# Gated attention in float32: weighted values as products over 32 rows, four heads side by side

## The chip, the cores and the metric

The kernel runs on one core of a Trainium2 chip. The metric is the device time of one execution in microseconds; of several runs the median is taken. TensorE is called PE in the profile (PEld for its weight loads), VectorE DVE, ScalarE ACT, GpSimd POOL, SyncE SP.

## The reference

Four batches of 512 tokens of width 256 go through a layer norm. An attention of 16 query heads over 4 key and value heads (head width 128, causal) and a feed-forward gate (inner width 1024) both read the normed tokens.

```python
xn = layernorm(x)
Q, K, V = xn @ Wq + bq, xn @ Wk + bk, xn @ Wv + bv          # 16, 4, 4 heads of 128
attn = softmax(Q K^T / sqrt(128) + causal mask)
y = gelu(concat_heads(attn @ V) @ Wo + bo)
s = layernorm(xn + y) * gamma + beta
gate, up = split(xn @ w_gate_up^T)
g = silu((silu(gate) * up) @ w_down^T)
out = x + s * g
```

All is float32. Query heads g, g + 4, g + 8, g + 12 share key head g.

## The kernel before, in words

Every float32 operand of TensorE is kept in two parts, hi (rounded) and lo (the exact rest), and a product is three matmuls, hi*hi, hi*lo and lo*hi, summed in PSUM (`product`, L93, its matmuls on L95, L96 and L97). `split_psum` (L82) makes the parts: hi by ACT (L86, or L89 with a bias), lo by DVE (L87, or L90).

The feed-forward gates of all four batches come first (`gate_up`, `down`); their results and the transposed tokens are parked in DRAM. The attention follows. It goes through 64 steps (batch b, key group g, query tile i of 128 queries). For a step, `scores` (L422) makes four tiles of scores: sub-tile t holds 32 queries of each of the four heads of the group on its 128 partitions, and as many keys as they see. DVE takes the negated, masked scores and their minimum out of PSUM (L449), ACT takes the exponential and its sum (L460), DVE the reciprocal of the sum (L473), and POOL scales (L474). `transposed_probs` (L476) turns the probabilities of key tile j on PE: four transposes (L481) into one PSUM bank, which ACT and DVE split (L86, L87) into pT, keys on the partitions. `weighted` (L486) then multiplies the values of key tile j, all 128 keys at once, with pT of four heads and 128 queries (512 columns) into the bank pc, and splits it into ctxT with the values' bias. `projected` (L505) multiplies ctxT by Wo into py, and at the end of a batch `activated` and `finished` do gelu, layer norm, gate and residual. For i = 0 the scores are a single matmul of whole float32 operands, q0 and k0 (`whole`, POOL, L373).

The order of the work is written out: each step collects chunks with a position (scores of the next step, queries of the next group, transposes and weighted values of this step, projection of the step before), sorts them, and emits them in that order. The planner of the framework starts on each engine the first instruction in that order that is ready by its own estimate, so an engine's queue can interleave neighbouring chunks, and from then on the queue is fixed. The last two steps are emitted side by side. All DMAs are issued on SP's queue, in order.

PSUM has eight banks: two for scores (tag "s"), two for transposes ("t"), one for queries, keys and values ("mm"), one for pc ("c"), two for py ("y0", "y1"). SBUF holds ten slots "w" for weights; the values stay in SBUF in two parts (tag "v").

Of the kernel before, what the change touches and what calls it, by code (L numbers as in the profile page):

```python
# [19 lines left out]
S = 32  # queries of a head in a tile of scores  # L20
MASK = -1e9
HIGHEST = 3.4028235e38
TUNE = {'a0': 0.119, 'a1': 0.3, 's0': 0.673, 's1': 0.335, 't0': 0.293, 't1': 0.231, 'w0': 0.519, 'w1': 0.5, 'o0': -0.076, 'o1': 0.537, 'gelu_at': (0, 1), 'gelu_pos': 0.0, 'fin_g': 1, 'fin_pos': 0.616, 'gelu_behind': 'ctx', 'qd': (1, 2, 1, 0), 'l0': 0.295, 'l1': 0.095, 'l2': 0.234, 'end': {'tab': -1.229, 'T1': 0.136, 'W1': 0.362, 'T0': 0.1, 'W0': 1.019, 'Ob': 0.072, 'Obs': 0.05, 'O1': 0.6, 'O1s': 0, 'O0': 1.0199999999999998, 'key': 'ctx', 'keyb': 'pT', 'G3': 0.1, 'F3': 0.101, 'Gb': 0.5, 'Fb': 0.65, 'vec': True}}
# [3 lines left out]
def kernel(  # L27
    ctx: ExitStack,
    tc: tile.TileContext,
    x: bass.AP,  # [B, L, D]  # L30
    wq: bass.AP,  # [D, H*E]
    bqT: bass.AP,  # [E, H]
    wk: bass.AP,  # [D, KV*E]
    bkT: bass.AP,  # [E, KV]
    wv: bass.AP,  # [D, KV*E]
    bvT: bass.AP,  # [E, KV]
    wo: bass.AP,  # [H*E, D]
    bo: bass.AP,  # [D]
    gamma: bass.AP,  # [D]
    beta: bass.AP,  # [D]  # L40
    wguT: bass.AP,  # [D, 2*INTER]
    wdT: bass.AP,  # [INTER, D]
    out: bass.AP,  # [B, L, D]
):
    """Products of float32 operands run on the tensor engine as products of two
    parts each: hi, rounded to the engine's 12 significant bits, and lo, the exact
    rest. hi*hi + hi*lo + lo*hi, summed in float32, is the float32 product."""
# [6 lines left out]
    G = H // KV  # query heads of a key head: g, g + KV, ...  # L54
    INTER = wdT.shape[0]
    NT = L // P  # token tiles of a batch
    ND = D // P  # chunks of the model dimension
    NI = INTER // P  # chunks of the inner dimension
# [10 lines left out]
    @contextmanager  # L69
    def behind(*keys):  # L70
        """Queues what the block does behind these instructions on their engines."""
        with ExitStack() as stack:
            for k in keys:
                for ins in latest[k]:
                    stack.enter_context(tc.issue_after(ins.ins))
            yield

# [4 lines left out]
    def split_psum(dst, src, bias=None):  # L82
        """dst[:, 0] = hi, dst[:, 1] = lo of a bank of PSUM (plus a bias per partition)."""
# [9 lines left out]
    def product(out_ap, lhs, rhs, first, last, **kw):  # L93
        """out += lhs^T rhs; lhs and rhs are (hi, lo)."""
        nc.tensor.matmul(out_ap, lhs[0], rhs[0], start=first, stop=False, **kw)  # L95
        nc.tensor.matmul(out_ap, lhs[0], rhs[1], start=False, stop=False, **kw)  # L96
        nc.tensor.matmul(out_ap, lhs[1], rhs[0], start=False, stop=last, **kw)  # L97

    # The power -1/2 of a variance.
    mhalf = const.tile([P, NT], F32, name="mhalf")  # L100
    nc.gpsimd.memset(mhalf, -0.5)
    # Loads the scalar engine's table before it is needed.
# [11 lines left out]
    def load_w(name, views, hi_on=None, lo_on=None):  # L114
        """A slot of 1024 columns of weights, in two parts."""
# [9 lines left out]
        w = work.tile([P, 2, 1024], F32R, tag="w", bufs=10, name=f"w_{name}")  # L125
# [6 lines left out]

    # Probabilities of a query tile: [32 queries of each head of a group, sub-tile of 32
    # queries, keys], the last key that the tile sees in the last column. What a sub-tile
    # doesn't see of the last P keys stays zero.
    p_tiles = [const.tile([P, NT, L], F32, name=f"p{k}") for k in range(2)]

    def clear(p, n):
        for t in range(NT - 1):
            nc.gpsimd.memset(p[:, t, ds(n - P + (t + 1) * S, P - (t + 1) * S)], 0.0)  # L140

    def load_x(b):
        if b < 2:
            t = work.tile([P, NT, D], F32, tag="xT", bufs=2, name=f"x_{b}")
        else:
            t = p_tiles[0][:, ts(b - 2, 2)].rearrange("p a n -> p (a n)").rearrange("p (t d) -> p t d", d=D)
# [9 lines left out]
    # The first tokens and the first weights come in small pieces, in the order of their use.  # L156
# [12 lines left out]
    w_first = work.tile([P, 2, 1024], F32R, tag="w", bufs=10, name="w_gu0")  # L169

    def split_first(f, lo_on=None):
        """The columns of f of the first slot of the gate's weights."""
# [8 lines left out]
    # Keeps the tensor engine busy until the first tokens are there, so that its clock is up by then.  # L181
# [22 lines left out]
    # What the attention phase wants back: the transposed tokens in two parts, and for  # L204
    # the end of a batch the normed tokens, gate * gamma and gate * beta + x.
    xT_dram = [dram.tile([P, ND, 2, L], F32, tag=f"xT{b}", name=f"xT_dram_{b}") for b in range(B)]
    fin_dram = [dram.tile([P, NT, 3, D], F32, tag=f"fin{b}", name=f"fin_dram_{b}") for b in range(B)]

    def normed(b, t):
        xn = work.tile([P, D], F32, tag="xn", bufs=2, name=f"xn_{b}_{t}")  # L210
# [8 lines left out]
    def transposed(b, t):  # L219
        """xT[b][c]: the normed tokens, transposed, of chunk c, in two parts."""  # L220
        if t == 0:
            xT[b] = [pair("pt", 4, f"xT_{b}_{c}") for c in range(ND)]
        xn = [normed(b, t), normed(b, t + 1)]
        pt = psum.tile([P, ND, 2, P], F32, tag="t", bufs=2, name=f"pxt_{b}_{t}")
# [27 lines left out]

    # The last S keys that a tile of scores sees hold the diagonal of each head. Masked
    # before the scores are scaled.
# [41 lines left out]
    ff_tags = [("s", 2), ("s", 2), ("t", 2), ("t", 2), ("mm", 1), ("c", 1)]  # L296
    def h_tiles(b):
        """Places for the eight tiles of a batch among those of the attention phase."""
        if b % 2 == 0 or b + 1 == B:
            for k in range(2 if b % 2 == 0 else 1):  # L300
                t = work.tile([P, G, 2, L], F32R, tag="q", bufs=2, name=f"hq_{b}_{k}")
                yield from (t[:, r] for r in range(G))
        else:
            yield from (pair("k", 4, f"hk_{b}_{k}") for k in range(4))
        if b % 2:
            yield from (pair("v", 5, f"hv_{b}_{k}") for k in range(4))
# [5 lines left out]
    def gate_up(b, f):  # L312
# [3 lines left out]
        for u in range(2):  # L316
            tags = ff_tags if b + 1 < B else ff_tags[:4]
            tag, bufs = tags[n_ff % len(tags)]
            n_ff += 1
            ps.append(psum.tile([P, L], F32, tag=tag, bufs=bufs, name=f"pg_{b}_{f}_{u}"))  # L320
# [15 lines left out]
        h = work.tile([P, L], F32, tag="ctx", bufs=2, name=f"h_{b}_{f}")  # L336
# [24 lines left out]
    kT, vv, qT, probs, pT, ctxT = {}, {}, {}, {}, {}, {}  # L361
    wqs, wos = {}, {}
    q0, k0 = {}, {}
    banks = ["mm", "c"]  # "c" only until the first values are weighted

    def free_bank():
        banks.append(banks.pop(0))
        return banks[-1]

    def whole(dst, t):  # L370
        """The first P columns as they were before they were split: so few columns go
        faster through the tensor engine whole."""
        nc.gpsimd.tensor_tensor(dst, t[:, 0].bitcast(F32), t[:, 1].bitcast(F32), ALU.add)  # L373

    def keys(b, g):
        pk = psum.tile([P, L], F32, tag=free_bank(), bufs=1, name=f"pk_{b}_{g}")
# [372 lines left out]
```

## Time and profile before

| | |
|---|---|
| median of three runs | 681.71 us (680.87 to 683.12) |
| span of the profiled execution, first to last instruction | 679.5 us |
| TensorE busy | 661.7 us, 3996 matmuls, mean granted clock 0.994 |
| VectorE, ScalarE, GpSimd busy | 447.8, 402.6, 273.4 us |
| DMA | 34.73 MB, 15.4% of 16 engines' span |

The page gives the span of the profiled execution; its own time is not listed apart from it, and what lies around the span is taken as the 2.2 us between the span and the median. Busy times are of one engine and overlap between engines. The feed-forward part fills the first 180 us, the attention the rest.

### The profile page before, as it was taken

To read this page: it belongs to the slowest core of one execution; us is meant where nothing else is said; L and a number is where in the kernel's file an instruction comes from. 1 tells how busy PE (TensorE), PEld (TensorE's weight loads), DVE (VectorE), ACT (ScalarE), POOL (GpSimd) and SP (SyncE) were. 2 spreads that over 40 slices of the span, in tenths; PEclk is the share of its full clock that TensorE was granted. 3 is DMA by queue.
4 is the path that set the end of the run, shared out by engine and by line. 5 is a ranking of instruction groups with operands and counts; after the bars stand their busy time and mean duration, and the time that the engine had idled before them with its cause. 6 is when DMAs were issued, how large, how long until landed. Compare 5 with 4: busy or idle time off the path is not lost.

```text
span 679.5 us, 12006 instructions
## 1 busy us (share of the span) xinstructions
PE 661.7 (97%) x3996; PEld 581.6 (86%) x3996; DVE 447.8 (66%) x1337; ACT 402.6 (59%) x956; POOL 273.4 (40%) x490
## 2 busy tenths in 40 slices
PE   7979999999999999999999999999999999999995
PEld 6768888889889888888888898889888988888984
DVE  5864434165766766775787666668867766687867
ACT  4434333253765766677676665957666668576772
POOL 5588130720646423222353232216433323354332
PEclk8999999999999999999999999999999999999998
DMA  7753322211310100000022000002210000032000
GB/s 223 246 191 122 127 81 90 77 47 50 92 31 2 36 29 1 1 0 1 20 76 94 1 0 1 2 1 63 63 62 1 1 2 1 1 93 79 1 1 32
DMA packets 25262, 34.73 MB, mean 51 GB/s; under 512 B 2288, under 2 KB 18544, under 8 KB 25200
## 3 DMA queue, kind: packets, MB, share of 16 engines
q1 hardware_dynamic: 25200, 33.97, 15.4%
q8 instruction: 31, 0.51, 0.3%
q14 instruction: 31, 0.25, 0.1%
HBM read 21.38 MB, written 12.58 MB: 50 GB/s over the span
## 4 chain that ended last, share of the span: by engine, by line
PE 89%; DVE 4%; DMA 4%; issue 1%; ACT 1%; POOL 1%; SPq 0%; ACTq 0%; DVEq 0%; POOLq 0%
PE pt L481 10%; PE pc L96 5%; PE pc L95 5%; PE pc L97 5%; PE pq L95 5%; PE py L97 4%; PE ps L97 4%; PE ps L96 4%; PE pq L97 4%; PE pq L96 4%; PE py L95 4%; PE ps L95 4%; PE py L96 4%; PE pg L97 3%; PE pg L96 3%; PE pg L95 3%
## 5 line engine op out<-in xcount | busy, mean ns | idle before, releaser
L474 POOL TENSOR_SCALAR p<-p,total 128x320 f32<-128x320 f32 (+15 forms) x256 | 127.6, 505 | 195.5 <-DVE total L473 174.9
L460 ACT ACTIVATE p<-p,least 128x320 f32<-128x320 f32 (+15 forms) x256 | 133.2, 522 | 59.7 <-DVE least L449 51.0
L449 DVE CUSTOM_DVE_ANT_0 p<-ps,mask 128x320 f32<-128x320 f32 (+15 forms) x256 | 109.8, 435 | 42.6 <-PE ps L97 17.5
L86 ACT CAST pT<-pt 128x512 fp32r<-128x512 f32 x160 | 89.2, 587 | 60.0 <-PE pt L481 59.2
L87 DVE TENSOR_TENSOR pT<-pt,pT 128x512 fp32r<-128x512 f32 x160 | 106.6, 686 | 25.5 <-ACT pT L86 25.0
L481 PE MATMUL pt<-ident,p 128*128 128x128 f32 x640 | 107.2, 273 | 0.5 <-POOL p L474 0.5
L481 PEld LDWEIGHTS pt<-ident,p 128*128 128x128 f32 x640 | 81.1, 142 | 17.5 <-POOL p L474 0.7
L97 PE MATMUL py<-w_o,ctxT 128*128 128x256 f32 x256 | 73.5, 287 | 0.6 <-DVE ctxT L90 0.6
L95 PE MATMUL py<-w_o,ctxT 128*128 128x256 f32 x256 | 72.9, 285 | 0.1
L96 PE MATMUL py<-w_o,ctxT 128*128 128x256 f32 x256 | 72.1, 281 | 0.0
L96 PE MATMUL pc<-pT,v 128*128 128x512 f32 x160 | 69.1, 432 | 0.0
L95 PE MATMUL ps<-kT,qT 128*128 128x288 f32 (+3 forms) x192 | 68.5, 357 | 0.0
L373 POOL TENSOR_TENSOR q<-qT 128x128 f32<-128x128 f32 x64 | 30.4, 474 | 93.7 <-DVE qT L90 55.8
L95 PE MATMUL pc<-pT,v 128*128 128x512 f32 x160 | 64.5, 403 | 0.1
L97 PE MATMUL pc<-pT,v 128*128 128x512 f32 x160 | 63.2, 395 | 0.0
L473 DVE RECIPROCAL total<-total 128x1 f32<-128x1 f32 x256 | 38.4, 158 | 37.2 <-ACT p L460 35.1
L96 PE MATMUL ps<-kT,qT 128*128 128x288 f32 (+3 forms) x192 | 62.2, 324 | 0.0
L97 PE MATMUL ps<-kT,qT 128*128 128x288 f32 (+3 forms) x192 | 61.7, 322 | 0.0
L90 DVE SCALAR_TENSOR_TENSOR qT<-pq,bq_sb,qT 128x512 fp32r<-128x512 f32 x64 | 47.9, 748 | 15.3 <-ACT qT L89 15.3
L89 ACT ACTIVATE qT<-pq,bq_sb 128x512 fp32r<-128x512 f32 x64 | 44.0, 687 | 20.1 <-PE pq L97 19.6
L90 DVE SCALAR_TENSOR_TENSOR ctxT<-pc,bv_sb,ctxT 128x512 fp32r<-128x512 f32 x64 | 47.8, 747 | 11.1 <-ACT ctxT L89 10.5
L95 PE MATMUL pg<-xT,w_gu 128*128 128x512 f32 (+1 forms) x132 | 50.5, 397 | 3.9 <-DVE h L338 2.5
(127 smaller groups left out, 1567.5 us busy)
## 6 DMA issues: line engine op xcount, KB each, us to landing
fin<-fin_dram SPq DMA_DIRECT2D x16, 384.0 KB, 3.2
xT_dram<-xT SPq DMA_DIRECT2D x8, 512.0 KB, 2.6
fin_dram<-gate SPq DMA_DIRECT2D x16, 256.0 KB, 2.0
xT_again<-xT_dram SPq DMA_DIRECT2D x8, 512.0 KB, 3.9
fin_dram<-xn SPq DMA_DIRECT2D x16, 128.0 KB, 2.4
st_q<-in_wq_dram SPq DMA_DIRECT2D x8, 256.0 KB, 3.2
st_o<-in_wo_dram SPq DMA_DIRECT2D x4, 512.0 KB, 3.9
out_dram<-y SPq DMA_DIRECT2D x16, 128.0 KB, 1.7
```

What stands on the lines that cost most here:

```text
L86: first = nc.scalar.copy(hi, src)
L87: second = nc.vector.tensor_tensor(lo, src, hi.bitcast(F32), ALU.subtract)
L89: first = nc.scalar.activation(hi, src, AF.Identity, bias=bias)
L90: second = nc.vector.scalar_tensor_tensor(lo, src, bias, hi.bitcast(F32), ALU.add, ALU.subtract)
L95: nc.tensor.matmul(out_ap, lhs[0], rhs[0], start=first, stop=False, **kw)
L96: nc.tensor.matmul(out_ap, lhs[0], rhs[1], start=False, stop=False, **kw)
L97: nc.tensor.matmul(out_ap, lhs[1], rhs[0], start=False, stop=last, **kw)
L449: nc.vector.tensor_tensor_reduce(pr, ps[:, :seen], mask[:, L - seen :], scale=-SCALE, scalar=HIGHEST, op0=ALU.add, op1=ALU.min, accum_out= ...
L460: exp = nc.scalar.activation(pr, pr, AF.Exp, bias=least[:, r : r + 1], scale=-1.0, accum_out=total[:, r : r + 1],)
L473: latest["dve"] = [nc.vector.reciprocal(total[:, r : r + 1], total[:, r : r + 1])]
L474: latest["pool"] = [nc.gpsimd.tensor_scalar(pr, pr, total[:, r : r + 1], 1.0, ALU.mult, ALU.mult)]
L481: nc.tensor.transpose(pt[:, :, t], p[:, t, ts(j, P)], ident)
```

## The change

The weighted values are computed without a transpose on PE. DVE turns each 32x32 block of a probability tile in its place, so that the 32 partitions of head r hold 32 keys of head r, with queries as columns. A matmul for one head then contracts over the 32 partitions of that head only, in row group r of the array, and the four heads of the group stand in the four row groups, each with its own PSUM bank. A key tile of 128 keys needs four such chunks c. The values have to lie on the partitions in the same way: 32 keys, the same for each of the four row groups. So they are written to DRAM (`v_dram`) and read back four times, once to each 32 partitions (`values_beside`).

Query tiles are handled in pairs: a step is (b, g, h), with tiles 2h and 2h + 1, and a matmul has 256 columns where both tiles see the key tile and 128 where only the second does. A weighted block has 96 matmuls for h = 0 and 192 for h = 1, all emitted as one chunk.

What moves with it: hi of the turned probabilities is an ACT copy from SBUF, lo is on POOL except for three of ten (i, j), which stay on DVE. The reciprocal is taken once for four sub-tiles and the scaling follows it. q0 comes from PSUM by ACT, and the split of queries covers 384 columns. The probabilities have a place for each query tile index (`p_tiles`). PSUM: the four banks "c" hold the weighted values of both halves; scores, queries, keys and values share the two banks "s". SBUF: twelve slots "w", which also take V beside each other and most of pT; Wq and Wo of a group are split once in batch 0, written to DRAM and read back in the later batches. The last two steps are no longer emitted side by side. Comments and the table of tuned positions are dropped; positions are constants.

```diff
+ON_DVE = ((1, 1), (3, 2), (3, 3))
...
+    banks = psum.tile([P, G, 2, 2 * P], F32, tag="c", bufs=1, name="banks")
...
     def values(b, t):
-        pv = psum.tile([P, KV * E], F32, tag=free_bank(), bufs=1, name=f"pv_{b}_{t}")
+        pv = psum.tile([P, KV * E], F32, tag="s", bufs=2, name=f"pv_{b}_{t}")
...
-        v = pair("v", 5, f"v_{b}_{t}")
+        v = pair("pt", 5, f"v_{b}_{t}")
         split_psum(v, pv)
-        vv[b, t] = v
+        nc.sync.dma_start(
+            v_dram[b][:, ts(t, P)].rearrange("g p s e -> p s g e"),
+            v.bitcast(F32).rearrange("p s (g e) -> p s g e", g=KV),
+        )
+
+    def values_beside(b, g, h):
+        n = L // S // 2
+        vr[b, g, h] = work.tile([P, n, 2, E], F32R, tag="w", bufs=12, name=f"vr_{b}_{g}_{h}")
+        for r in range(G):
+            nc.sync.dma_start(
+                vr[b, g, h][ts(r, S)].rearrange("p c s e -> p c (s e)").bitcast(F32),
+                v_dram[b][g, ts(h, L // 2)].rearrange("(c k) s e -> k c (s e)", k=S),
+            )
...
+        pq = pq.rearrange("p (t n) -> p t n", n=S)
+        nc.scalar.activation(q0[b, g][:, :, r], pq[:, :NT], AF.Identity, bias=bq_sb[:, h : h + 1])
+        split_psum(qT[b, g][:, :, :, r], pq[:, NT:], bq_sb[:, h : h + 1])
...
-        latest["dve"] = [nc.vector.reciprocal(total[:, r : r + 1], total[:, r : r + 1])]
-        latest["pool"] = [nc.gpsimd.tensor_scalar(pr, pr, total[:, r : r + 1], 1.0, ALU.mult, ALU.mult)]
+        if t == G - 1:
+            latest["dve"] = [nc.vector.reciprocal(total, total)]
+            for k in range(NT):
+                normalized(b, g, i, k)
...
     def transposed_probs(b, g, i, j):
         p = probs[b, g, i][0]
-        pt = psum.tile([P, G, NT, S], F32, tag="t", bufs=2, name=f"pt_{b}_{g}_{i}_{j}")
-        for t in range(NT):
-            nc.tensor.transpose(pt[:, :, t], p[:, t, ts(j, P)], ident)
-        t = pair("pt", 4, f"pT_{b}_{g}_{i}_{j}")
-        latest["pT"] = split_psum(t, pt.rearrange("p r t n -> p (r t n)"))[:1]
-        pT[b, g, i, j] = t
...
+        u = work.tile([P, NT, NT, S], F32, tag="u", bufs=3, name=f"pu_{b}_{g}_{i}_{j}")
+        nc.vector.transpose(u, p[:, :, ts(j, P)].rearrange("p t (c k) -> p c t k", k=S))
+        u = u.rearrange("p c t q -> p c (t q)")
+        h = i // 2
+        both = j < 2 * h + 1
...
+        t = pT[b, g, h, j][:, :, :, i % 2 if both else 0]
+        nc.scalar.copy(t[:, 0], u)
+        lo_on = nc.vector if (i, j) in ON_DVE else nc.gpsimd
+        lo_on.tensor_tensor(t[:, 1], u, t[:, 0].bitcast(F32), ALU.subtract)
+
+    def weighted(b, g, h):
+        for j in range(2 * h + 2):
+            t = pT.pop((b, g, h, j))
+            v = vr[b, g, j // 2]
+            first = 0 if j < 2 * h + 1 else 1
+            for c in range(NT):
+                for a, d in ((0, 0), (0, 1), (1, 0)):
+                    for r in range(G):
+                        nc.tensor.matmul(
+                            banks[:, r, h, first * P :],
+                            v[ts(r, S), (j % 2) * NT + c, a],
+                            t[ts(r, S), d, c].rearrange("p i n -> p (i n)"),
+                            start=j == 0 and c == 0 and a == d,
+                            stop=c == NT - 1 and a == 1 and j >= 2 * h,
+                            skip_group_check=True,
+                            tile_position=(r * S, 0),
+                        )
...
+    steps = [(b, g, h) for b in range(B) for g in range(KV) for h in range(2)]
+    steps[-2:] = reversed(steps[-2:])
...
+        if n == 0 and ph + 1 < NPH:
+            for r in range(G):
+                chunks.append((0.05 + 0.15 * r, queries, (*divmod(ph + 1, KV), r)))
+        if n == 1 and ph + 2 < NPH:
+            chunks.append((0.45, keys, divmod(ph + 2, KV)))
...
+                    chunks.append((0.0 + 0.3 * m + 0.075 * t, scores, (nb, ng, i, t)))
+            for m, (i, j) in enumerate(transposed_all[steps[s + 1]]):
+                chunks.append((0.65 + 0.35 * m / len(transposed_all[steps[s + 1]]), transposed_probs, (nb, ng, i, j)))
+        chunks.append((0.7, weighted, (b, g, h)))
+        if n == 1 and ph + 1 < NPH:
+            for m in range(2):
+                chunks.append((0.71, values_beside, (*divmod(ph + 1, KV), m)))
...
+                    chunks.append((0.08 + 0.3 * m + 0.075 * r, projected, (pb, pg, i, r)))
...
+    nc.scalar.activation(warm, mhalf[:, 0:1], AF.Gelu)
+    activated(B - 1, [2, 3])
+    for t in (2, 3):
+        finished(B - 1, t, False)
+    for t in (0, 1):
+        load_fin(B - 1, t)
+        for r in range(G):
+            projected(B - 1, KV - 1, t, r)
+    for t in (0, 1):
+        activated(B - 1, [t])
+        finished(B - 1, t, True)
```

## The prediction

> **What bounds the kernel now.** I read the table of engines first, then the slices, then the windows by stage, then the waits of TensorE, then its timeline.
>
> ```profile
> PE 661.7 (97%) x3996; PEld 581.6 (86%) x3996; DVE 447.8 (66%) x1337; ACT 402.6 (59%) x956; POOL 273.4 (40%) x490
> ...
> PE   7979999999999999999999999999999999999995
> ...
> PEclk8999999999999999999999999999999999999998
> ```
> ```profile
> 180.00:660.00 480.00, 478.94 (x2967) 424.00 (x2966) 340.24 (x1108) 324.79 (x800) 186.18 (x366) 1.00 0.08 25
> ```
> In the window of the attention phase the columns after the length are PE, PEld, DVE, ACT, POOL, clock, DMA share. TensorE (PE) is busy 478.94 of 480 us at full clock; DVE has 71%, ACT 68%, POOL 39%, DMA 8%. So a microsecond taken from PE's stream is worth a microsecond, up to some 140 us, when DVE would be next.
>
> ```profile
> PE pg L95 <- DVE h L338: 2.5, 1, 2.5
> ...
> PE pt L481 <- POOL p L474: 0.5, 1, 0.5
> ```
> These are the waits of PE (total, times, longest): nothing of the attention phase keeps it waiting over 1 us. Any wait that the change adds is a net loss.
>
> A busy PE is not PE's rate, since a matmul lasts longer than the distance to the next. The timeline (start, duration) gives the distances:
>
> ```profile
> 520.18 0.28 PE L95 MATMUL py<-w_o,ctxT 128*128 128x256 f32 x1
> 520.30 0.28 PE L96 MATMUL py<-w_o,ctxT 128*128 128x256 f32 x1
> 520.42 0.28 PE L97 MATMUL py<-w_o,ctxT 128*128 128x256 f32 x1
> 520.54 0.60 PE L481 MATMUL pt<-ident,p 128*128 128x128 f32 x4
> 520.89 0.47 PE L96 MATMUL pc<-pT,v 128*128 128x512 f32 x1
> 521.21 0.40 PE L97 MATMUL pc<-pT,v 128*128 128x512 f32 x1
> 521.44 0.40 PE L95 MATMUL pc<-pT,v 128*128 128x512 f32 x1
> ```
> ```profile
> 545.78 0.27 PE L481 MATMUL pt<-ident,p 128*128 128x128 f32 x1
> 545.81 0.48 PE L95 MATMUL pc<-pT,v 128*128 128x512 f32 x1
> ```
> A 512-wide product takes 0.23 us from start to start, a 256-wide one 0.12 (0.118 over longer stretches), a transpose 0.11 (0.60 for four whose last lasts 0.27). The shortest distance is the last pair: 0.03 us.
>
> **What PE loses.** 640 transposes (L481) by 0.11 are 70 us; the chain's share of 10% of the span says 68. The weighted values (pc) are 480 matmuls by 0.232, 111 us. Together 181 us go.
>
> **What PE gets.** Per key group and batch (16 of them) the first pair of query tiles takes 48 matmuls 256 wide and 48 of 128, the second 144 and 48; in all 3072 and 1536, or 1152 sets of four row groups, 768 wide and 384 narrow. A set multiplies as much as one old matmul of its width: the gain is the transposes alone, if four run as one. No row shows 32 rows. From below: a set costs as much as one full-height matmul, 0.118 or, for narrow ones, 0.11 as transposes do: 90.6 + 42.2 = 133 us, 48 us gained. From above: each matmul with its weight load stands for itself, four times that, 531 us, 350 us lost. Between: the 0.03 row says that a fourth matmul starts 0.09 us after the first, so a set that must end before the next starts lasts 0.118 + 0.09 = 0.21, one that overlaps freely 0.118. I take the middle, 0.16 a set: 184 us, **+3 us against the 181 removed**. PE's work stays as it is, and the transposes' gain is spent on four times the instructions.
>
> The Trainium skill bears on this twice. TensorE: Matmul & The Clock Gate, "Measured speedup vs the span model", gives 3.07 times for four row tiles of 512 columns; with 0.118 that would be 0.154 a set and an estimate of 177 us, 4 us gained. The same page, "The mechanism", says that a weight load overlaps running matmuls only where the row groups differ. If so, a row group's next load (0.11) would follow its own matmul (0.118), 0.23 a wide and 0.22 a narrow set and an estimate of 260 us, 79 us lost. In this trace 256-wide matmuls of all 128 rows follow each other at 0.118, each with a load that lasts 0.19 in the records, so loads do run under matmuls of the same rows; no row here shows either case for 32 rows.
>
> **Changes of shape on PE.** Products of 32 and of 128 rows now alternate. After transposes the first product (0.47 long) delays the next to 0.32 instead of 0.23, but it starts 0.03 after the last transpose instead of 0.11, which makes up for it: no loss. That is the lower end, 0. The upper end is that PE runs empty, 0.28 long less 0.118, 0.16 us a change. Twice a step are 64 changes. But the timeline shows single pc matmuls put between other products, so 300 are possible, 48 us. I take 64 by 0.16, **+10 us**.
>
> **Banks.** Queries, keys, values and scores now share the two banks "s"; before, scores had two and the others one or two. A query's bank is held after its last matmul by the ACT copy of q0 (nearest row: exp of 128x128, 403 ns), by hi on 384 columns (exp 384: 618 ns) and by lo on DVE (748 ns for 512, so some 580): 1.6 us. Meanwhile the other bank lets one score (0.42) and a projection (three times 0.118) run: 0.8 us are uncovered, 64 times, 51 us. What can cover them are the weighted products, if their probabilities are there: then 0. Before, a query held its bank for 0.687 + 0.748 = 1.4 us and no wait of pq is on PE's list, because something else was always ready. I take a third, **+17 us**; ends 0 and 51.
>
> **Other engines.** All in the attention window, against its 480 us. DVE: 112 lo of probabilities by 686 ns go to POOL (-77), 192 reciprocals by 158 (-30), a quarter of 64 qT by 748 (-12); 160 transposes of 32x32 blocks come, priced by the row of the same size from SBUF (w_gu on L112, 680 ns): +109. Bounds: 290 ns (the 128x128 reduction) to 1.05 us (hk on L343), 46 to 168; so 267 to 389 busy, under PE. ACT: probabilities from SBUF cost 620 (row L342) for 587, +5; q0 +26, shorter hi -11: 345. POOL: 64 q0 sums by 474 go (-30), 112 lo by 1.35 us come (w_q on L112): +151, 307. In the first batch splits of weights add four rows a slot, 2 by 0.68 and 2 by 1.4, as now. None is the bound. Probabilities are prepared a step ahead, some 15 us, over DVE, ACT and POOL (0.68 + 0.62 + 1.35 us a block); that step covers them, and I cost them at nothing. Without it the last tile's chain (four by 0.68 on DVE, then 0.62 and 1.35: 4.7 us) would be seen 16 times: 75 us. The single reciprocal makes four normalizations wait for the last exp; they stand in the same cover.
>
> **DMA.** Values go to DRAM and come back beside each other (16 writes of 0.5 MB, 128 reads of 0.25), weights go and come (8 and 24 of 1 MB): 75 MB, at the 246 GB/s of an early slice 307 us spread over 480. A half of V is 1 MB, 4 us, asked for one step ahead. All are issued on SP's queue in order, behind out, fin and reload, and behind weights that wait for a slot. At the start values need out (2.6 us) and back (3.9) before the first weighted product; queries and scores cover most: **+2 us**; ends 0 and 6.
>
> **The end.** Before, the last two steps ran side by side. Now the last weighted block (24 sets, 3.8 us) has little beside it, and projections, gelu and the layer norm of two tiles follow: **+4 us**; ends -2 and 10.
>
> **Sum.** 3 + 10 + 17 + 2 + 4 = +36 on the span of 679.5: 715.5. What lies around the span is 2.2 us (median 681.7), so 717.7, rounded to **717**.
>
> **Rivals.** *Full overlap, and covered waits.* Sets at 0.118, weighted products fill the banks' waits; changes of shape (10), start and end (6) stay: 679.5 - 48 + 16 = 647.5, around 650 in all, and 676 if the banks' waits are half seen. For it: matmuls may start 0.03 apart, and loads hide under matmuls now. Against: no row shows 32-row loads side by side, and PE's list has no slack to give.
> *Weight loads in a line.* On the other side of the bill: PEld is 86% busy with 3996 loads; the change makes it 7484. Loads 0.11 apart are the shortest stream that transposes show. If four row groups' loads share one path, a set costs 0.44 and all sets 507 us, 326 more, with the other terms 1041 us in all; where two overlap, 0.22 and 253 us, +72, in all near 787. It decides from 0.2 us a set on. The case in which the row positions bring nothing ends here too.
> *V comes late.* SP's list has out waiting 418.9 us for the layer norm, up to 101.7 at once; nothing urgent stands behind it now, but V's halves would. If each of the 32 halves came 2 us late, +64, with the rest near 780.
>
> **How the numbers follow.** Forecast (684 to 760) 0.42; full overlap 0.27; loads in a line 0.19; late V 0.09; within 0.3% of before, which is what a measurement of this kernel can tell from none, 0.03. Faster 0.27, same 0.03, slower 0.70. For 8 in 10 the range starts at 648, which leaves out a third of the full overlap (0.09), and ends at 815, which leaves out the half of the second rival with sets over some 0.24 (0.10). The forecast's own range is 684 to 760.
>
> **What would show it.** Right: sets of four pc matmuls start to start near 0.16 us; PE below 97%, with waits of ps and pq for DVE or ACT; POOL near 390 us busy over the span, DVE unchanged. Wrong: sets at 0.12 and PE still full (the first rival), PEld over 90% with sets over 0.2 (the second), pc waiting for DMA (the third), or DVE's transposes over 1 us.

## The result and the profile after

The changed kernel takes 873.28 us (median of 4 runs, 871.32 to 877.21), against 682.01 for the kernel before: a ratio of 1.282 (95% interval 1.278 to 1.286). The prediction was 717 with a range of 648 to 815. The profiled execution has a span of 869.0 us; before it was 679.5, so 189.5 us have come. Engines and slices of the kernel after:

```profile
PE 740.1 (85%) x7484; PEld 608.3 (70%) x7484; DVE 481.6 (55%) x1193; ACT 422.8 (49%) x1021; POOL 389.9 (45%) x535
...
PE   7899999982978998989869979798798898987864
...
PEclk9999999996997997899989999999799898998977
```
```profile
180.00:860.00 680.00, 569.08 (x6547) 461.28 (x6547) 390.40 (x999) 355.72 (x892) 316.77 (x430) 0.92 0.44 121
```
The second is the window of the attention phase: after the length PE, PEld, DVE, ACT, POOL, clock, DMA share and GB/s. No engine is full. TensorE waits 111 us in this window, and its mean clock is 0.92 where it was 1.00. TensorE's waits (total, times, longest) name DVE first; the list begins:

```profile
PE ps L465 <- DVE least L476: 27.5, 13, 16.2
PE py L97 <- DVE ctxT L554: 21.8, 16, 4.7
PE banks L539 <- ACT pT L525: 14.3, 12, 3.1
PE ps L95 <- DVE least L476: 13.1, 14, 6.6
```
Added up over the list, 45 of the 111 us end with a score reduction ("least", which frees a bank "s"), 31 with the two parts of the weighted values (ctxT, which the projection needs), 16 with turned probabilities (pT) and 14 with lo of queries (qT), which frees a bank too.

The weighted products themselves run well. One stretch of TensorE's timeline (start, duration):

```profile
524.49 0.28 PE L97 MATMUL ps<-kT,qT 128*128 128x256 f32 x1
524.70 3.95 PE L539 MATMUL banks<-pT,vr 32*128 32x256 f32 x126
528.58 0.40 PE L95 MATMUL ps<-kT,qT 128*128 128x288 f32 x1
```
126 matmuls in 3.88 us to the next start, 0.031 each, 0.123 for a set of four with the change at its end: a set costs about what one full-height matmul of 256 columns costs (0.118).

To see where 189.5 us came from I added up the distances from the start of each matmul to the next, from 180 us on, and set each against the shortest distance that matmuls of its width show (0.118 us for 256 columns, a quarter of it in the row groups). The first line is the change in these shortest distances, the others what lies above them.

| | before | after | change |
|---|---|---|---|
| shortest distances of all matmuls | 491.9 | 446.6 | -45 |
| TensorE waiting | 1.6 | 110.9 | +109 |
| distances next to a wait | 2 | 22 | +20 |
| at half clock: excess | 0 | 35 | +35 |
| at changes between 32 and 128 rows | 0 | 41 | +41 |
| other distances: products of 128 rows; of 32 rows | -3.4; 0 | 19; 7 | +29 |

The changed kernel switches to 32-row products 180 times ("stretches" below).

### The profile page after: what moved, and what is told of

It is laid out like the page before. It is cut to its first block, busy times and chain, and to the rows that moved or that the text cites. A ratio compares the mean times of both kernels' runs of the same rounds, so it can differ in the third digit from the quotient of the medians.

```text
span 869.0 us, 18724 instructions
## 1 busy us (share of the span) xinstructions
PE 740.1 (85%) x7484; PEld 608.3 (70%) x7484; DVE 481.6 (55%) x1193; ACT 422.8 (49%) x1021; POOL 389.9 (45%) x535
## 4 chain that ended last, share of the span: by engine, by line
PE 38%; POOL 18%; issue 16%; DVE 14%; ACT 9%; DMA 4%; SPq 0%; POOLq 0%; ACTq 0%; DVEq 0%
POOL p L506 10%; DVE pu L514 5%; POOL pT L527 5%; ACT pT L525 4%; PE banks L539 3%; DVE pT L527 3%; PE banks L95 2%; PE ps L95 2%; PE banks L97 2%; PE banks L96 2%; PE py L97 2%; PE pd L96 2%; PE pd L95 2%; PE pq L95 2%; PE pd L97 2%
## 5 line engine op out<-in xcount | busy, mean ns | idle before, releaser
L506 POOL TENSOR_SCALAR p<-p,total 128x288 f32<-128x288 f32 (+15 forms) x256 | 127.2, 516 | 262.1 <-DVE total L499 258.3
L539 PEld LDWEIGHTS banks<-pT,vr 32*128 32x128 f32 x4608 | 159.9, 190 | 66.3 <-issue 42.3
L539 PE MATMUL banks<-pT,vr 32*128 32x256 f32 (+1 forms) x4608 | 191.9, 291 | 15.9 <-ACT pT L525 14.3
L487 ACT ACTIVATE p<-p,least 128x288 f32<-128x288 f32 (+15 forms) x256 | 132.4, 518 | 121.0 <-DVE least L476 109.6
L527 POOL TENSOR_TENSOR pT<-pu,pT 128x512 fp32r<-128x512 f32 x112 | 147.7, 1337 | 68.7 <-ACT pT L525 68.5
L476 DVE CUSTOM_DVE_ANT_0 p<-ps,mask 128x288 f32<-128x288 f32 (+15 forms) x256 | 108.4, 431 | 75.5 <-PE ps L97 63.7
L525 ACT CAST pT<-pu 128x512 fp32r<-128x512 f32 x160 | 96.5, 619 | 101.9 <-DVE pu L514 101.0
L514 DVE STREAM_TRANSPOSE pu<-p 128x512 f32<-128x512 f32 x160 | 103.6, 687 | 73.5 <-POOL p L506 73.1
L95 PE MATMUL ps<-kT,qT 128*128 128x160 f32 (+2 forms) x192 | 76.8, 400 | 20.8 <-DVE least L476 13.1
L97 PEld LDWEIGHTS py<-w_o,ctxT 128*128 128x128 f32 x256 | 52.8, 206 | 28.0 <-DVE ctxT L554 27.6
L96 PE MATMUL ps<-kT,qT 128*128 128x160 f32 (+2 forms) x192 | 64.1, 334 | 0.0
L95 PEld LDWEIGHTS py<-w_o,ctxT 128*128 128x128 f32 x256 | 53.5, 209 | 14.5 <-ACT ctxT L553 14.1
L97 PE MATMUL ps<-kT,qT 128*128 128x160 f32 (+2 forms) x192 | 63.6, 331 | 0.0
```

What stands on the lines that cost most here:

```text
L476: nc.vector.tensor_tensor_reduce(pr, ps[:, :seen], mask[:, L - seen :], scale=-SCALE, scalar=HIGHEST, op0=ALU.add, op1=ALU.min, accum_out= ...
L487: exp = nc.scalar.activation(pr, pr, AF.Exp, bias=least[:, r : r + 1], scale=-1.0, accum_out=total[:, r : r + 1],)
L506: latest["pool"] = [nc.gpsimd.tensor_scalar(pr, pr, total[:, t : t + 1], 1.0, ALU.mult, ALU.mult)]
L514: nc.vector.transpose(u, p[:, :, ts(j, P)].rearrange("p t (c k) -> p c t k", k=S))
L525: nc.scalar.copy(t[:, 0], u)
L527: lo_on.tensor_tensor(t[:, 1], u, t[:, 0].bitcast(F32), ALU.subtract)
```

## The experiments

The theories: **shape**, each change between products of 32 and of 128 rows costs time; **DVE's order**, the turns stand in DVE's queue ahead of score reductions and hold them back; **POOL's hold**, lo on POOL slows lo on DVE; **banks**, two banks for everything is too few; **the planner**, constants as positions give a bad order. The expectations name theories by letters and say what each letter stands for; theory D is DVE's order. "Waiting" is TensorE's idle time from 180 us on, counted as in the table.

**e1, one matmul of all 128 rows for each set.**
```diff
-for r in range(G):
-    nc.tensor.matmul(banks[:, r, h, first * P :], v[ts(r, S), (j % 2) * NT + c, a],
-                     t[ts(r, S), d, c]..., tile_position=(r * S, 0))
+nc.tensor.matmul(banks[:, c, h, first * P :], v[:, (j % 2) * NT + c, a], t[:, d, c]...)
```


> The changed kernel with each set of four 32-row matmuls replaced by one matmul over all 128 rows of the same operands and width (1152 instead of 4608; the weighted values then mix the heads, so the result is left wrong). PE streams as many columns as with sets of 0.118 us. Theory A (the four-row-group shape itself and the order that the planner makes for it, in which it reckons 32-row matmuls one after another): the 41 us at changes of shape and a good part of the 111 us of idle PE go, 710 to 760 us. Theory B (two banks for scores, queries, keys and values, and DVE held up by POOL, make the waits): only the changes of shape go, 820 to 840 us.

754.8 us (ratio 1.107, 1.102 to 1.111), 118 less than the change. This is in theory A's range. Distances at changes between weighted and other products go from 41 us to about 1, but waiting falls too, from 111 to 66, and the time at half clock from 109 to 55. The planner puts the queue together differently with fewer instructions (89 stretches for 180), so this is the price of the shape with all that follows from it.

**e2 and e3, lo of the turned probabilities all on POOL, all on DVE.**
```diff
-ON_DVE = ((1, 1), (3, 2), (3, 3))
+ON_DVE = ()                                                       # e2
+ON_DVE = tuple((i, j) for i in range(4) for j in range(4))        # e3
```


> The changed kernel with the lo parts of all probabilities on POOL and none on DVE (48 move). In the changed kernel these 48 take 1.25 us in the mean and 7.6 us at worst on DVE, while POOL subtracts. If DVE held up by POOL (theory B) makes much of PE's idle time: 800 to 845 us. If the order is the cause (theory A): within 10 us of 873, as POOL only gets 64 us more to do.

> The changed kernel with the lo parts of all probabilities on DVE and none on POOL (112 move). DVE gets 112 by 0.69 = 77 us more, and only POOL's scaling and its splits of weights are left to hold it up. Theory B: the long holds go and POOL's chain is shorter, 800 to 850 us. Theory A: 865 to 900, DVE more loaded, same waits for banks.

869.5 (1.276, 1.270 to 1.281) and 884.4 us (1.296, 1.292 to 1.300). POOL's hold of DVE is real (last section), but with it taken away on either side the time moves by 1%: in this order of the queues it is not the cause.

**e4, the kernel before with the changed kernel's two banks**, for scores, queries, keys and values.
```diff
-pq = psum.tile([P, L], F32, tag=free_bank(), bufs=1, name=f"pq_{b}_{h}")      # pk, pv alike
+pq = psum.tile([P, L], F32, tag="s", bufs=2, name=f"pq_{b}_{h}")
```


> The kernel before with queries, keys and values in the two banks of the scores (tag s), all else as before; the other banks stay unused by them. The price of sharing by itself. If the two banks are a main cause of PE's idle time: 730 to 790 us. If they cost only where queues are badly ordered: 683 to 700 us.

699.5 us, 1.026 (1.024 to 1.029): 18 us, near the price that the prediction had put on it (17). The agreement is partly luck: TensorE's waiting grows by only 6 us there (2 to 8), the rest is longer distances, and the prediction had priced waits of the changed kernel.

**e5 and e6, the order of TensorE's products.** e5 keeps the emitted order on all engines; e6 keeps the planner but puts each step's weighted products, as one piece, behind the products emitted before them and ahead of those after.
```diff
-with tile.TileContext(nc, schedule_with_timeline_sim=True) as tc:
+with tile.TileContext(nc, schedule_with_timeline_sim=False) as tc:                     # e5
...
+            key = "pe" if f is weighted else "w"                                       # e6
+            with behind(key) if key in latest else nullcontext():
                 f(*a)
```


> The changed kernel, its engines' queues filled in the order of emission as far as slots allow, not by the planner's estimate of when an instruction is ready. PE then has 52 stretches of weighted products instead of 180. Theory A (the order that the planner makes): of the 41 us at changes of shape two thirds go, and PE waits for DVE less, 780 to 830 us. Theory C (DVE's queue has the turning of probabilities in front of the reductions that free the banks, and these wait for POOL's scaling): the waits remain or grow, 860 to 930.

> The changed kernel with each step's weighted block in one piece on PE: it is queued behind the products emitted before it, and those emitted after it behind it; 32 stretches instead of 180. Changes of shape cost 41 us for 180 stretches, so 34 us should go. Theory A: the waits stay as they are or shrink a little, 820 to 845 us. Theory C, in which the weighted products are what fills PE's waits for the banks: the waits grow as much as the changes save, 860 to 900.

883.6 (1.296, 1.294 to 1.298) and 877.2 us (1.287, 1.284 to 1.290). The changes nearly vanish (52 and 32 stretches, 9 and 8 us), and waiting grows by more (161 and 174, from 111). Fewer changes alone bring nothing: what they give back is lost again in waits.

**e7, POOL's scaling of probabilities left out**, which leaves POOL 111 us less to do and the turns nothing to wait for on POOL.
```diff
-            for k in range(NT):
-                normalized(b, g, i, k)
+            latest["pool"] = [nc.gpsimd.tensor_scalar(total, total, 1.0, 1.0, ALU.mult, ALU.mult)]
```


> The changed kernel without POOL's scaling of the probabilities (256 instructions, 127 us on POOL, are left out; the weighted values stay unscaled, so the result is left wrong). The turning on DVE then waits for ACT's exp alone. Theory C: the 73 us in which DVE's queue stands before a turn for POOL, and with it most of PE's waits, go: 770 to 810 us. Theory A: the waits for banks remain, 840 to 870.

822.0 us (1.202, 1.196 to 1.209), between the two ranges: waiting falls to 61, and what of it ends with a score reduction from 45 to 20. What DVE's turns wait for reaches TensorE.

**e12, scaling on DVE** instead. What was queued behind POOL's scaling (loads of weights, the layer norm at the end of a batch) no longer is.
```diff
-        latest["pool"] = [nc.gpsimd.tensor_scalar(pr, pr, total[:, t : t + 1], 1.0, ALU.mult, ALU.mult)]
+        nc.vector.tensor_scalar(pr, pr, total[:, t : t + 1], 1.0, ALU.mult, ALU.mult)
```


> The changed kernel with the scaling of the probabilities on DVE instead of POOL (256 instructions move), so a turn on DVE waits for no other engine after the reciprocal. The 73 us in which DVE stands before a turn for POOL go, and up to 127 us are added to DVE's 482. Theory C, with the handoff to POOL as the longest link: 800 to 840 us. If DVE's load decides: 880 to 920.

866.4 us (1.270, 1.265 to 1.274), waiting 93, between the two ranges. A handover between engines less helps by 7 us; the turns are still ahead of the reductions.

**e8, turns one step later**, at 0 to 0.4 of the step that uses them. In one late step of the 32, scores overwrite probabilities before they are turned.
```diff
-                chunks.append((0.65 + 0.35 * m / len(...), transposed_probs, (nb, ng, i, j)))
+                chunks.append((0.0 + 0.4 * m / len(...), transposed_probs, (b, g, i, j)))
```


> The changed kernel with the probabilities of a step turned at the front of the step itself (positions 0 to 0.4) and not at the end of the step before (0.65 to 1.0). POOL has then long scaled them, so DVE's queue should not stand. Theory C: 800 to 840 us. Theory A: 860 to 890, since the weighted products get their operands later and fill fewer gaps.

878.9 us (1.288, 1.283 to 1.293). This place alone brings nothing.

**e9 and e10, a deeper loop**: scores of the next step, turns of this step, weighted products of the step before; in e10 these in one piece as in e6.
```diff
+            for m, (i, j) in enumerate(transposed_all[steps[s]]):
+                chunks.append((0.0 + 0.6 * m / len(...), transposed_probs, (*steps[s][:2], i, j)))
+        if 1 <= s <= N:
+            chunks.append((0.7, weighted, steps[s - 1]))
```


> The changed kernel with one step more between the stages: in the loop of step s PE makes the scores of s + 1, DVE turns s, the weighted products are those of s - 1, the projection that of s - 2; the last two steps in plain order. Each handoff then has a step more. Theory C (PE waits because the chain of scores, exp, scaling, turn and split of one step is longer than the step): PE's idle time falls from 111 to under 50 us, the changes of shape stay, 760 to 810 us. Theory B (two banks): 850 to 880.

> The same deeper pipeline, with the weighted block of s - 1 at the front of the step and in one piece on PE (47 stretches instead of 180). Theory C: neither the changes of shape (41 us) nor most of the idle time are left, 680 to 740 us. Theory B: the weighted products no longer fill the waits for the banks, so what the changes give is lost there, 800 to 880.

986.9 (1.446, 1.443 to 1.450) and 865.8 us (1.268, 1.265 to 1.271): e9 is slower than either theory had it, e10 lies in the range of two banks. In the free order of e9 a whole step of lead makes it worse: TensorE waits 186 us, and the lists say for whom:

```profile
PE ps L465 <- DVE least L476: 97.2, 12, 11.8
```
```profile
DVE pu L514 <- POOL p L506: 116.0, 57, 4.4
```
The first is the largest of TensorE's waits in e9, scores that want a bank; the second is the largest of DVE's, a turn that wants scaled probabilities. No wait for turned probabilities (pT) is on TensorE's list of e9, so these are not too late for the weighted products; what stands behind the turn in DVE's queue is late. Added up over the trace, TensorE waits 129 us for score reductions in e9, and during 113 of them DVE is turning, subtracting lo or waiting to do so. In the change the same sum is 34 of 45 us. That trace shows one such case from end to end (start, duration; idle before and its releaser in brackets):

```profile
194.89 0.66 PE L465 MATMUL ps<-k,q 128*128 128x32 f32 x4
...
199.30 1.90 DVE L514 STREAM_TRANSPOSE pu<-p 128x512 f32<-128x512 f32 x3 [4.39 <-POOL p L506]
...
201.88 7.59 DVE L527 TENSOR_TENSOR pT<-pu,pT 128x512 fp32r<-128x512 f32 x1 [0.68 <-ACT pT L525]
...
209.51 0.71 DVE L514 STREAM_TRANSPOSE pu<-p 128x512 f32<-128x512 f32 x1
...
210.91 0.69 DVE L527 TENSOR_TENSOR pT<-pu,pT 128x512 fp32r<-128x512 f32 x1 [0.69 <-ACT pT L525]
...
211.52 0.18 DVE L476 CUSTOM_DVE_ANT_0 p<-ps,mask 128x32 f32<-128x32 f32 x1
...
211.76 0.74 PE L465 MATMUL ps<-k,q 128*128 128x96 f32 x2 [16.22 <-DVE least L476]
```
Two scores are done at 195.55 and hold both "s" banks. The reduction that would free the first lasts 0.18 us, but it stands behind turns that wait 4.39 us for POOL, behind a lo that takes 7.59 and another turn and lo. TensorE waits 16.22 us; this is the longest case of all.

**e11, the kernel before without its hand-set positions.**
```diff
-TUNE = {'a0': 0.119, ...}
+TUNE = {}
```


> The kernel before with its table of positions emptied, so that the defaults of the code place the chunks: what hand-set places are worth where PE has transposes and four banks more. If the loss comes from the coarse order of the changed kernel as such: 710 to 760 us. If PE's queue forgives an order as long as banks are there: 682 to 695.

687.7 us, 1.009 (1.007 to 1.011): constants as positions cost 6 us there, with four banks more. So lost tuning by itself is not a loss of this size; a tuned order of the changed kernel was not tried.

**e13 to e16, DVE's order mended.** All four put each turn behind the score reduction emitted last in DVE's queue:
```diff
-        nc.vector.tensor_tensor_reduce(...)
+        latest["red"] = [nc.vector.tensor_tensor_reduce(...)]
...
-        nc.vector.transpose(u, ...)
+        with behind("red"):
+            nc.vector.transpose(u, ...)
```
e13 is this in e10, with turns at 0.3 to 0.9 and weighted products at 0.5 of a step; e14 in the change itself, with the turns a step later as in e8, at 0.3 to 0.6; e15 is e13 with all lo on POOL; e16 is e13 without the one piece, so e9 with the rule and these positions.

> The deeper pipeline with one rule for DVE's queue: a turn is queued behind the last reduction of scores emitted before it (turns at 0.3 to 0.9 of the step, the weighted block of the step before in one piece at 0.5). In the deeper run before, PE waited 108 us for score reductions that stood in DVE's queue behind turns, which waited for POOL's scaling. Theory D (this order on DVE, with two banks, is the wait): PE's idle time in the attention under 60 us, the span 700 to 760 us. Theory E (the chain is too long for the step however the queues are ordered, or the two banks alone hold PE): 830 to 880.

> The changed kernel with the same rule for DVE's queue and no other depth: turns in their own step at 0.3 to 0.6, weighted products at 0.7 (in one late step scores overwrite probabilities before they are turned, so a part of the result is left wrong). Theory D with the order alone: 760 to 820. Theory E: 860 to 900, since the weighted products then wait for the turns.

> As the deeper pipeline with turns behind reductions, and all lo parts on POOL, so that no subtraction with both operands in SBUF stands in DVE's queue during POOL's work. Theory D: 5 to 20 us faster than with three of ten on DVE, if their holds (7.6 us at worst) sit before reductions; the same within 5 us if not.

> As the deeper pipeline with turns behind reductions, but PE's weighted products are not held in one piece (249 stretches). At 0.31 us a change, some 215 stretches more cost 65 us, and the planner moves scores ahead: 40 to 90 us slower than in one piece under theories D and E alike.

836.0 (1.225, 1.222 to 1.228), 804.0 (1.179, 1.175 to 1.184), 806.4 (1.182, 1.178 to 1.187) and 817.4 us (1.196, 1.187 to 1.204).

e14 is 69 us faster than the change, while e8 without the rule lost 6. But the gain does not come where theory D put it. Waiting falls only from 111 to 90, and what ends with a score reduction stays (46 us for 45):

```profile
PE ps L95 <- DVE least L476: 20.0, 27, 3.5
PE ps L465 <- DVE least L476: 15.2, 3, 5.1
...
PE py L97 <- DVE ctxT L555: 4.1, 12, 1.6
```
During these 46 us DVE spends 9 on turns, lo and waits for them, where it was 34; most of the rest are reductions (17) and the layer norm. Waits of the projection fall from 31 to 6. The larger part of the 69 is fewer changes, 63 stretches for 180 (15 us for 41), other distances 16 us shorter and 10 us less excess at half clock. Why the planner changes less often under the rule is not shown.

e13 falls into theory E's range (830 to 880) and not into theory D's: with the weighted products in one piece TensorE waits 105 us, 56 of them for score reductions, and then DVE is mostly at reductions (35 us) and little at turns and lo (12). So here the order of the turns is no longer what holds TensorE; the two banks are what theory E names. With lo on POOL, e15, 29.5 us go, more than the 5 to 20 expected: with the order mended the place of lo counts. And e16, in the free order, is 19 us faster than e13, where 40 to 90 slower was expected.

The rule shows best between e9 and e16, 169 us. Waiting falls from 186 to 43 us, and what ends with a score reduction from 129 to 19; the list of TensorE's waits begins

```profile
PE ps L95 <- DVE qT L90: 13.2, 16, 3.0
PE ps L95 <- DVE least L476: 9.2, 9, 2.3
```
and DVE's wait for POOL's scaling, 116.0 us in e9, is

```profile
DVE pu L515 <- POOL p L506: 3.0, 1, 3.0
```
The positions were moved along with the rule, so 169 is the price of both, and so is e14's 69: e8's turns stand at 0 to 0.4 of the step, e14's at 0.3 to 0.6. What is left in e16 is changes: 249 stretches, 62 us at their edges.

```profile
493.07 0.40 PE L97 MATMUL pq<-xT_again,w_q 128*128 128x512 f32 x1
493.40 0.39 PE L540 MATMUL banks<-pT,vr 32*128 32x256 f32 x4
493.72 0.44 PE L95 MATMUL ps<-kT,qT 128*128 128x384 f32 x1
494.00 0.34 PE L96 MATMUL ps<-kT,qT 128*128 128x384 f32 x1
494.17 0.34 PE L97 MATMUL ps<-kT,qT 128*128 128x384 f32 x1
```
A single set between two 128-row products, in e16 at full clock: 0.33 us into it where a 512-wide product takes 0.23, 0.32 for the set where it needs 0.117, and 0.28 for the first product after where the next takes 0.17. That is 0.41 us for one set's visit.

**e17 and e18, what is left.** e17 is e16 with e1's matmuls of 128 rows; e18 is e15 with the weighted products in 2 or 4 pieces a step, one for a key tile.
```diff
-            chunks.append((0.5, weighted, steps[s - 1]))
+            k = 2 * steps[s - 1][2] + 2                                        # e18
+            for j in range(k):
+                chunks.append((0.1 + 0.7 * j / k, weighted, (*steps[s - 1], j)))
```


> e16 (turns behind the score reductions, a free order of TensorE's products) with each set of four 32-row matmuls replaced by one matmul of all 128 rows of the same width: 1152 instead of 4608, no change of shape left, heads mixed in the output. Sets cost the same nominally (0.117 us). If changes of shape are what remains in e16 (its distances around them are 62 us over the nominal ones, those of the weighted products among themselves 12 more, and the half clock that follows some of them), it takes 715 to 750 us, and TensorE's idle time stays near e16's 43 us. If the wait for probabilities and banks remains and only shows itself at the changes, idle time grows by what the changes give back, and it takes 790 us or more.

> e15 (one stretch of weighted products a step, behind all earlier products, idle 95 us, 32 stretches) with each step's weighted products put into 2 or 4 pieces, one for a key tile, at positions 0.1 to 0.8 of the step, each in one stretch: about 98 stretches. If idle time comes from a whole step's weighted products standing apart from the scores that wait for the banks, the pieces fill those waits: idle falls to about 65 us while 66 more changes at 0.31 us cost 20, so 780 to 800 us. If a fixed order is the cost, since every piece is a place where the queue waits for its probabilities, it takes 806 us or more.

738.9 (1.082, 1.076 to 1.088) and 859.8 us (1.260, 1.256 to 1.265). e17 lands where the shape theory put it, 79 us under e16, although waiting is a little longer (61 us for 43): the distances of sets and changes shrink from 87 us over the shortest to 7, those among the 128-row products from 39 to 13, half clock included. Its queue is again put together differently (119 stretches). e18 misses its 780 to 800: 98 stretches in a fixed order make waiting longer (115 us for 95) and not shorter. Its list of waits names the two parts of the weighted values (ctxT) for 57 us, score reductions for 26 and turned probabilities (pT) not at all, so it is not for these that the pieces wait. Its half clock lasts 133 us until the last matmul, e15's 68. So a fixed order costs waits and a free one costs changes; of the kernels that keep the 32-row products none reaches the 682 of before.

## Why the prediction was wrong

The direction held (slower): TensorE was full, and any wait that the change added was a loss. Its size did not: the sum was +36, the measurement +189.5. Term by term:

**Sets, 184 us taken for 181 removed.** 131 us by the shortest distances, 142 with what stands above them inside the stretches, half clock included, against some 176 removed. This was the lower end (133), the first rival's rate: 45 us gained where a loss of 3 was forecast. Two sentences of the Trainium skill were weighed there. TensorE: Matmul & The Clock Gate, "The mechanism", lets a load overlap only where row groups differ and made 0.22 to 0.23 us of a set (the same section also has loads pulled ahead into a background weight buffer, which the prediction did not weigh); this trace says 0.114 to 0.123 on average (131 and 142 over 1152), so the inference that each row group's next load waits for its own matmul does not hold. "Measured speedup vs the span model" with 3.07 times made 0.154; here a set of four takes about as long as one product of 128 rows, which would be close to 4 times if a single 32-row product took that long too; no run has one alone. The rival of loads in a line, with its 787 to 1041 us, has nothing in the runs: PEld fell from 86% to 70%, and that 873 lies between the two is chance.

**Changes of shape, 64 by 0.16 us: +10.** This step failed twice. There were 180 stretches, 360 changes, since the planner spreads the sets between other products; and a stretch costs 0.23 us at its two edges (41 us over 180) and some 0.34 with the distances just around it (7 among the sets, and 13 of the 19 us among 128-row products, since e17 without changes shows 6: 61 over 180). 41 to 61 against 10; the named upper end, 48, was nearer, but rested on one change costing 0.16 and did not count the product after it. The Trainium skill has the rule that I did not look for, in TensorEngine Tiling (Array Packing), "Key Properties": a change of tiling mode drains the array. The 0.33, 0.32 and 0.28 above agree with it; it gives no price.

**Probabilities "are prepared a step ahead ... and I cost them at nothing".** This is the step that failed most. The cover was mostly there for the weighted products (they waited 16 us for pT, against 75 without cover), but I asked only who waits for the turned probabilities, not what is queued behind a turn. On DVE that is the reduction which frees a score's bank, and with two banks TensorE has little else to do: 45 us of waiting end with a reduction, and during 34 of them DVE is at turns, lo or the waits for them. e7, e9 and e16 show this path at work.

**Other waits.** Waiting came to 109 us more and distances next to a wait to 20, of which 23 were in the sum (banks 17, start 2, end 4) and 106 were not. The banks' term was near: 14 us end with lo of queries, the hold that it described. 31 us end with the two parts of the weighted values, for which the projection had no term at all; e14 cuts them to 6, and how much of them comes from DVE's order stays open.

**Half clock: no term.** 109 us of the attention ran at half clock before the last matmul, +35. It mostly follows waits of about 2 us (last section); I wrote that every wait is a net loss and gave it no second price.

**What held.** The turn was priced 680 ns and takes 687; POOL was to be near 390 us busy and is 389.9. DVE was not to be the bound and is not, but its busy time was to fall by 10 us (340 to 330 in the window) and rose by 34 over the span: the 48 lo left on it take 1.25 us each where 0.69 was priced, 27 us in all. V beside each other lands in 5.6 us, and the weight loads of the weighted products wait 0.2 us for it in all, so the third rival is out. The sum by these measurements: 36 - 53 (sets) + 5 (removed work) + 60 (changes and other distances, 70 for 10) + 106 (waits) + 35 (half clock) = 189. The terms are measured; how far each causes the others is not, since waits bring half clock and the order of the queue moves waits and changes together.

What stays open: the share of the changed order in e1 and e17, since the planner's queue moves with the number of instructions, and the share of the rule in e14's 69, of which only 20 are waiting. That e14's 69 and e1's 118 nearly add up to the loss shows nothing: no run has both in this kernel, and they overlap.

## What to carry to other kernels

When work moves from a full engine to one that is half idle, look at the order of the receiving queue: what stands behind the new instruction, what that frees, and how many buffers the full engine has until then. Slack in busy time (DVE 55%) and a whole step of lead didn't help; turns queued behind the reductions, at another place of the step, gave back 69 us, and 169 in the deeper loop. Products over 32 rows ran at full rate in long stretches (0.123 us a set of four); count the stretches, at 0.3 to 0.4 us each here with what stands around them, before the matmuls. And a time that matches a rival's range (873 in 787 to 1041) doesn't make the rival right: its sign, PEld over 90%, was absent.

## What the runs showed of the hardware

**Half clock after short waits.** In the change's attention phase the clock fell to half 15 times before the last matmul, for 3.41 us or a multiple of it (up to 17.07). In 13 of the 15 cases TensorE had stood still for 1.9 to 3.0 of the 3.41 us before, in one wait or several (in the other two for 0.8 and 1.0). One case, on TensorE's timeline and in two windows:

```profile
671.18 0.50 PE L95 MATMUL pv<-w_v,xT_again 128*128 128x512 f32 x1 [2.29 <-DVE qT L90]
...
672.95 0.48 PE L539 MATMUL banks<-pT,vr 32*128 32x128 f32 x4
673.36 0.77 PE L95 MATMUL ps<-kT,qT 128*128 128x480 f32 x1
673.93 0.60 PE L96 MATMUL ps<-kT,qT 128*128 128x480 f32 x1
```
```profile
669.00:672.40 3.40, 1.22 (x5) 1.05 (x6) 1.18 (x4) 2.18 (x6) 3.32 (x3) 1.00 0.00 0
672.50:679.30 6.80, 6.80 (x24) 4.68 (x23) 2.11 (x4) 2.81 (x7) 0.00 (x0) 0.50 0.26 77
```
A wait of 2.29 us is followed by 6.8 us at clock 0.50 (third column from the end), in which TensorE is busy throughout. An equal wait of 2.29 us, ending at 503.15, was followed by none. The trace shows the difference: all 15 starts lie on one grid of 3.41 us. On this grid the harmless wait falls into two intervals, 0.95 and 1.34 us, the harmful one into one, 2.11 us. Every interval at full clock with 1.85 us of standing still or more was followed by half clock, and of those with 1.34 us or less only two were (the 0.8 and 1.0).

**A subtraction on DVE held for 7.59 us.** In the timeline of e9's section, lo of 128x512 with both inputs in SBUF lasts 7.59 us on DVE, from 201.88 on, while POOL does six subtractions of 1.25 us one after another, four of them parts of weights:

```profile
201.57 2.48 POOL L112 TENSOR_TENSOR w_o<-st_o,w_o 128x512 fp32r<-128x512 f32 x2
...
204.01 1.26 POOL L527 TENSOR_TENSOR pT<-pu,pT 128x512 fp32r<-128x512 f32 x1
...
205.23 1.26 POOL L112 TENSOR_TENSOR w_q<-st_q,w_q 128x512 fp32r<-128x512 f32 x1
206.45 1.26 POOL L527 TENSOR_TENSOR pT<-pu,pT 128x512 fp32r<-128x512 f32 x1
207.67 1.25 POOL L112 TENSOR_TENSOR w_q<-st_q,w_q 128x512 fp32r<-128x512 f32 x1
```
The median of the 48 lo on DVE is 0.75 us; one more took 7.07. The Trainium skill, SBUF — State Buffer, "Who interferes with whom", says that a VectorE instruction with two SBUF inputs contends with a GpSimd instruction that reads SBUF, and that the order of issue decides which of the two blocks. That agrees in kind; that the hold spans several of POOL's instructions is what the trace adds.
